# Layer 1's blocks with themselves: a quarter of the scores turned by TensorE, empty places filled, and an end of its own for the last block

## The chip, the cores and the metric

The kernel runs on one core of a Trainium2 chip. The metric is device time in microseconds (us) from the first to the last instruction of one execution; the time of a kernel is the median of its runs. The core's engines work side by side: TensorE (PE) multiplies, and loads weights on a path of its own (PEld); VectorE (DVE), ScalarE (ACT) and GpSimd (POOL) work element by element; transfers are issued on SyncE's queue (SP). Each engine takes its instructions in the order in which the program was built, and waits where one needs what another engine has not yet delivered.

## The reference, cut to what matters

The input x has 4 images of 128 channels and 64 x 64 = 4096 places. Layer 0 is an attention with keys and queries of 64 channels and a gate; layer 1, which the change touches, takes the result as 4096 tokens of 128 channels, attends with queries that are also the keys, and ends in a recurrent step over the tokens.

```python
def _L1_attn_ref(x, W, b):
    q = jnp.einsum('bsd,de->bse', x, W)
    scores = jnp.einsum('bsd,btd->bst', q, q)      # symmetric: q with itself
    attn = jax.nn.softmax(scores, axis=-1)
    return jnp.einsum('bst,btd->bsd', attn, x)

def _L1_ffn_ref(x, W, V, gamma, beta):
    Wx = jnp.einsum('bti,hi->bth', x, W)
    flat = Wx.reshape(B * T, H)                    # mean and variance over all tokens of all images
    mean = jnp.mean(flat, axis=0); var = jnp.var(flat, axis=0)
    Wx = ((flat - mean) * jax.lax.rsqrt(var + BN_EPS) * gamma + beta).reshape(B, T, H)
    def step(yt, wx_t):
        yt = jax.nn.sigmoid(wx_t + yt @ V.T)
        return (yt, yt)
    ...

# layer 0
x = x + _L0_conv_ref(_gn(x), ...)
# layer 1
t = _to_tokens(x)
t = t + _L1_attn_ref(_ln_t(t), L1_attn_W, L1_attn_b)
t = t + _L1_ffn_ref(_ln_t(t), L1_ffn_W, L1_ffn_V, L1_ffn_gamma, L1_ffn_beta)
```

Since layer 1's scores are symmetric, the kernel works out a block of 512 keys by 512 queries once and turns its exponentials for the opposite block. A block with itself holds the same twofold content within the one block.

## The kernel before

The core holds P = 128 partitions; a block has QB = 512 places (NQ = 4 tiles of 128), and there are NB = 8 blocks per image. Small work is cut into steps in two queues: `pending` holds what finishes a block, `ahead` what prepares the next image. In layer 0 the loop takes `ahead` first, and `pending` every second time:

```python
def nothing():
    pass
# ... attention, the loop of layer 0: per pair of key tiles
if ahead:
    ahead.popleft()()
elif pending and (p % 2 == 0 or len(pending) > 6):
    pending.popleft()()
```

Layer 1 goes through blocks n of queries and a <= n of keys. `slots` takes the row sums, one column for each block n; `quarter` and the tile `before` do not exist yet. The blocks with a < n are turned by VectorE and transfers, and used a second time by `reversed_products`:

```python
slots = accp.tile([P, NT, NB], F32, tag="slots", name="slots", bufs=2)
# ...
def order(n):
    return [0, 1] if b == B - 1 and n == 0 else list(range(n, -1, -1))
# ...
def direct():
    n, a, i, e, o = fifo.popleft()
    for half in range(2):
        nc.tensor.matmul(
            o, lhsT=h[:, NQ * a + 2 * i + half, :], rhs=e[:, half, :],
            start=(a == order(n)[0] and i == 0 and half == 0),
            stop=(a == order(n)[-1] and i == 1 and half == 1),
        )
    if a == order(n)[-1] and i == 1:
        part(n, o)
# ...
for n in [NB - 2, NB - 1] + list(range(NB - 3, -1, -1)):
    # ...
    for a in order(n):
        # ...
        for i in range(2):
            ps = ps_s.tile([P, 2, QB], F32, tag="s", name="ps")
            e = ep.tile([P, 2, QB], F32, tag="e", name="e")
            for half in range(2):
                at = NQ * a + 2 * i + half
                nc.tensor.matmul(
                    ps[:, half, :], lhsT=qt[:, bass.ts(at, P)],
                    rhs=qt[:, bass.ts(n, QB)], start=True, stop=True,
                )
            for half in range(2):
                at = NQ * a + 2 * i + half
                nc.scalar.activation(
                    e[:, half, :], ps[:, half, :], AF.Exp, bias=shift,
                    accum_out=slots[:, at, n : n + 1],
                )
                if turns(n, a):
                    nc.vector.transpose(
                        d.rearrange("q f b k j -> q k b f j")[:, 2 * i + half],
                        e[:, half, :].rearrange("q (b f j) -> q b f j", b=NQ, f=NQ),
                    )
            if o is None:
                o = ps_o.tile([P, QB], F32, tag="o", name="o")
            if n == NB - 2 and i == 0 and a > 0:
                queries(a - 1)
            elif n == NB - 2 and a == 0 and i == 1:
                flush((b, NB - 1))
                queries(NB - 1)
            fifo.append((n, a, i, e, o))
            clock += 1
            if len(fifo) > LAG:
                direct()
                if a == n and i == 0:
                    direct()
            if turned and turned[0][0] <= clock:
                reversed_products()
            if pending:
                pending.popleft()()
            elif ahead:
                ahead.popleft()()
        # ... the transfers that turn d into t, and turned.append((clock + 4, n, a, t))
    while fifo:
        direct()
```

A block is finished when all its parts are there. `ps_m` has one bank, so the steps below follow one another on it:

```python
def finish(n):
    cs = bass.ts(n, QB)
    rinv = stat.tile([P, NQ], F32, tag="rinv", name="rinv")
    t = work.tile([P, 4, NQ, 32], F32, tag="t", name="t1", bufs=2)
    h2 = work.tile([P, NQ, C], F32, tag="h2", name="h2")
    th = work.tile([P, QB], F32, tag="th", name="th")
    t1 = work.tile([P, NQ, C], F32, tag="og", name="t1b")
    nc.sync.dma_start(t, t_d[b, n])
    def tokens():
        at = (B + b) * NT + n * NQ
        den = den_all[:, at : at + NQ]
        nc.vector.tensor_reduce(den, slots[:, bass.ts(n, NQ), :], AX.X, ALU.add)
        nc.vector.reciprocal(rinv, den)
        m = ps_m.tile([P, NQ, P], F32, tag="m", name="mt")
        for j in range(NQ):
            nc.tensor.transpose(m[:, j, :], oacc[:, n, bass.ts(j, P)], ident)
        for j in range(NQ):
            nc.vector.scalar_tensor_tensor(
                t1[:, j, :].rearrange("q (p i) -> q p i", p=4),
                m[:, j, :].rearrange("q (p i) -> q p i", p=4), rinv[:, j : j + 1],
                t[:, :, j, :], ALU.mult, ALU.add,
            )
        layernorm(quarters(t1), quarters(h2))
    def result():
        m = ps_m.tile([P, QB], F32, tag="m", name="mr")
        for j in range(NQ):
            nc.tensor.transpose(m[:, bass.ts(j, P)], t1[:, j, :], ident)
        t2 = work.tile([P, QB], F32, tag="xb", name="t2")
        nc.scalar.copy(t2, m)
        nc.sync.dma_start(t2_d[b, :, cs], t2)
    def turn():
        m = ps_m.tile([P, QB], F32, tag="m", name="mh")
        for j in range(NQ):
            nc.tensor.transpose(m[:, bass.ts(j, P)], h2[:, j, :], ident)
        nc.scalar.copy(th, m)
    def inputs():
        m = ps_m.tile([P, QB], F32, tag="m", name="mw")
        nc.tensor.matmul(m, lhsT=wt["f"], rhs=th, start=True, stop=True)
        nc.vector.bn_stats(bn_st[:, b * NB + n, :], m)
        m = m.rearrange("p (g i s) -> p i g s", i=L // 2, s=2)
        # ... copied to wxs, or to DRAM for the images before the last
    if b == B - 1 and n == 0:
        pending.extend([tokens, turn, inputs, result])
    else:
        pending.extend([tokens, result, turn, inputs])
```

After the last block the statistics of all tokens are joined, and the recurrent step runs over 32 groups' starts in parallel. The pool `scan` takes the place in memory of what stood there before:

```python
        flush()
# ...
    with ExitStack() as st:
        scan = st.enter_context(tc.tile_pool(name="scan", bufs=1))
        # ... loads of t2, tiles y and state, first products into the banks of ps_r (line 725)
mv = scan.tile([P, 2], F32, name="bn_mv")
nc.vector.bn_aggr(mv, bn_st.rearrange("p a b -> p (a b)"))
gain = scan.tile([P, 1], F32, name="gain")
inv_sqrt(gain, mv[:, 1:2], EPS_BN)
nc.vector.tensor_mul(gain, gain, col(GAMMA))
bias = scan.tile([P, 1], F32, name="bias")
nc.vector.tensor_mul(bias, mv[:, 0:1], gain)
nc.vector.tensor_sub(bias, col(BETA), bias)
# ...
                nc.scalar.activation(dst, at(wxs, i, bs), AF.Sigmoid, bias=bias, scale=gain)   # line 761
```

## Time and profile before

| What | Value |
|---|---|
| time, median of 3 runs (lowest, highest) | 3108.49 us (3106.8, 3109.73) |
| span of the profiled execution, mean granted clock of TensorE | 3106.2 us, 0.993 |
| GpSimd | 5% busy |
| one 512-column exponential of layer 1 (ScalarE), its read-out of the row sum | 684 ns, 196 ns |
| layer 1 of the second image, 1134 to 1530 us: see the slices from 1200 to 1500, TensorE busy | 98.05 to 98.90 us of each 100 |
| the last slice, 3000 to 3100: TensorE busy, granted clock | 61.80 us of 100, 0.82 |
| chain that ended last: layer 0's products, its scores | 28%, 15% |
| the same: layer 1's scores, direct products, turned products | 15%, 14%, 12% |

How to read the lines that follow: a group shows line, engine, operation, tile written and tiles read, shapes and count, then busy time and the mean duration of one in ns, then the engine's idle time just before it and what ended it. In the timeline the first number is the start in us, the second the length of the piece, and the bracket gives idle time before it with what ended it. TensorE's instructions overlap, and their ends are modelled, so the distance of two starts says more than a duration.

### The profile page before, as it was taken

What the parts mean: (1) busy time and instruction counts of PE and PEld (TensorE: products, weight loads), DVE (VectorE), ACT (ScalarE), POOL (GpSimd) and SP (SyncE); (2) the same over time, 40 slices, a digit from 0 to 9 for tenths busy, and PEclk for the clock granted to TensorE, in tenths of its full rate; (3) what the DMA queues carried; (4) which work ended last, traced back from release to release, by engine and by line L of the source; (5) the groups of instructions that cost most, each with busy time, mean ns of one, the idle gap of its engine ahead of it and who ended that gap; (6) DMA issues with size and microseconds to landing.
All of it is one profiled execution on the core that took longest, in us unless ns stands there. A gap on an engine that the chain in (4) does not pass through costs nothing.

```text
span 3106.2 us, 32252 instructions
## 1 busy us (share of the span) xinstructions
PE 3018.6 (97%) x10706; PEld 1362.3 (44%) x10706; DVE 1877.7 (60%) x3160; ACT 1144.8 (37%) x2018; POOL 144.5 (5%) x183
## 2 busy tenths in 40 slices
PE   7999999999999999999999999999999999999976
PEld 3444444444444444444444444444444444444432
DVE  6666656555666665655566666555566666455546
ACT  3444433333344443333334443333334444323324
POOL 0000000000000000000000000000000000000000
PEclk9999999999999999999999999999999999999988
DMA  1011143333111123334211114333321113443423
GB/s 51 28 55 55 55 111 88 91 89 92 46 55 55 55 78 93 90 89 97 73 52 55 50 43 116 88 91 93 91 56 55 49 44 121 114 104 88 98 98 157
DMA packets 233168, 241.14 MB, mean 78 GB/s; under 512 B 88480, under 2 KB 144288, under 8 KB 231968
## 3 DMA queue, kind: packets, MB, share of 16 engines
q1 hardware_dynamic: 231984, 238.18, 28.2%
q8 instruction: 88, 1.44, 0.2%
q10 hardware_dynamic: 1008, 0.79, 0.1%
q14 instruction: 88, 0.72, 0.1%
HBM read 65.80 MB, written 56.62 MB: 39 GB/s over the span
## 4 chain that ended last, share of the span: by engine, by line
PE 91%; DVE 4%; SPq 1%; POOL 1%; DMA 1%; issue 1%; ACT 0%; ACTq 0%; DVEq 0%; POOLq 0%
PE o L394 28%; PE ps L215 15%; PE ps L613 15%; PE o L501 14%; PE ot L514 12%; SPq L650 1%; PE m L243 1%; PE mw L582 1%; PE mq L487 1%; PE mp L326 1%; PE ps_r L764 1%; PE mh L577 1%; POOL rstd L132 1%; DVE t1b L559 1%; PE mp L361 1%; PE mp L346 1%
## 5 line engine op out<-in xcount | busy, mean ns | idle before, releaser
L394 PE MATMUL o<-e,nxt 64*128 64x512 f32 x4096 | 963.8, 589 | 0.0
L217 ACT ACTIVATE e<-ps 128x1024 f32<-128x1024 f32 x512 | 521.4, 1025 | 674.7 <-PE ps L215 657.5
L224 DVE TENSOR_TENSOR acc<-acc,e 128x1024 f32<-128x1024 f32 x448 | 547.6, 1222 | 236.4 <-ACT e L217 220.5
L619 ACT ACTIVATE e<-ps,shift 128x512 f32<-128x512 f32 x580 | 393.9, 684 | 749.8 <-PE ps L613 497.1
L394 PEld LDWEIGHTS o<-e,nxt 64*128 64x128 f32 x4096 | 399.0, 187 | 482.3 <-issue 474.5
L613 PE MATMUL ps<-qt 128*128 128x512 f32 x1160 | 547.8, 595 | 2.7 <-ACT qt L488 2.7
L501 PE MATMUL o<-e,h 128*128 128x512 f32 x1160 | 537.7, 592 | 0.0
L215 PE MATMUL ps<-nxt 64*128 64x512 f32 x2048 | 534.5, 596 | 1.2 <-DVE nxt L338 0.9
L514 PE MATMUL ot<-tt,h 128*128 128x512 f32 x888 | 399.8, 593 | 0.0
L624 DVE STREAM_TRANSPOSE dd<-e 128x512 f32<-128x512 f32 x444 | 286.5, 686 | 83.4 <-ACT e L619 73.1
L501 PEld LDWEIGHTS o<-e,h 128*128 128x128 f32 x1160 | 218.3, 191 | 260.7 <-issue 259.5
L613 PEld LDWEIGHTS ps<-qt 128*128 128x128 f32 x1160 | 213.4, 191 | 249.0 <-issue 224.2
L215 PEld LDWEIGHTS ps<-nxt 64*128 64x128 f32 x2048 | 194.5, 187 | 231.5 <-issue 158.8
L514 PEld LDWEIGHTS ot<-tt,h 128*128 128x128 f32 x888 | 167.9, 190 | 210.0 <-issue 205.7
L519 DVE TENSOR_REDUCE slots<-tt 128x4 f32<-128x2048 f32 x111 | 250.7, 2258 | 9.7 <-DMA tt<-dd 9.4
L528 DVE TENSOR_TENSOR oacc<-oacc,ot 128x512 f32<-128x512 f32 x87 | 59.3, 682 | 209.8 <-PE ot L514 209.8
L131 POOL TENSOR_SCALAR rstd<-mv 128x4 f32<-128x4 f32 x64 | 14.6, 228 | 2456.5 <-DVE mv L268 2456.5
L619 ACT ACTIVATION_READ_ACCUMULATOR e<-ps,shift 128x1 f32 x580 | 113.9, 196 | 0.0
L448 DVE SCALAR_TENSOR_TENSOR t<-yt,rinv,t 128x128 f32<-128x128 f32 x128 | 36.6, 347 | 71.5 <-DMA yt<-turn_d 71.4
L411 POOL TENSOR_SCALAR xb<-xb,bpc 128x512 f32<-128x512 f32 x32 | 57.4, 1793 | 318.0 <-DMA xb<-in_x_dram 289.3
L132 POOL TENSOR_TENSOR rstd<-rstd,mhalf 128x4 f32<-128x4 f32 x64 | 66.4, 1038 | 5.3
L271 DVE TENSOR_SCALAR h<-t,mv,rstd 128x128 f32<-128x128 f32 x128 | 35.7, 343 | 47.1 <-POOL rstd L132 47.1
(134 smaller groups left out, 1491.7 us busy)
## 6 DMA issues: line engine op xcount, KB each, us to landing
tt<-dd SPq DMA_DIRECT2D x1776, 64.0 KB, 2.0
turn_d<-d SPq DMA_DIRECT2D x96, 256.0 KB, 2.0
t_d<-t SPq DMA_DIRECT2D x64, 256.0 KB, 2.0
nxt<-in_x_dram SPq DMA_DIRECT2D x16, 512.0 KB, 5.5
xb<-in_x_dram SPq DMA_DIRECT2D x32, 256.0 KB, 2.9
t<-turn_d SPq DMA_DIRECT2D x128, 64.0 KB, 2.0
yt<-turn_d SPq DMA_DIRECT2D x128, 64.0 KB, 2.0
qt<-turn_d SPq DMA_DIRECT2D x128, 64.0 KB, 2.0
```

What stands on the lines that cost most here:

```text
L132: nc.gpsimd.tensor_tensor(dst, dst, mhalf[:, :n], ALU.pow)
L215: nc.tensor.matmul(ps[:, h, :], lhsT=lhsT, rhs=rhs, start=True, stop=True)
L217: nc.scalar.activation(e, ps, AF.Exp, scale=scale)
L224: nc.vector.tensor_tensor(acc, acc, e, ALU.add)
L394: nc.tensor.matmul(o[r], lhsT=v[rs, p + h * PAIRS, :], rhs=e[rs, h, :], start=(p == 0 and h == 0), stop=(p == PAIRS - 1 and h == 1),)
L501: nc.tensor.matmul(o, lhsT=h[:, NQ * a + 2 * i + half, :], rhs=e[:, half, :], start=(a == order(n)[0] and i == 0 and half == 0), stop=(a = ...
L514: nc.tensor.matmul(ot, lhsT=h[:, NQ * n + j, :], rhs=t[:, :, j, :, :].rearrange("q p k j -> q k p j"), start=(j == 0), stop=(j == NQ - 1),)
L519: nc.vector.tensor_reduce(slots[:, bass.ts(n, NQ), a], t.rearrange("q p b k j -> q b p (k j)"), AX.XY, ALU.add,)
L528: nc.vector.tensor_tensor(oacc[:, n, :], oacc[:, n, :], o, ALU.add)
L613: nc.tensor.matmul(ps[:, half, :], lhsT=qt[:, bass.ts(at, P)], rhs=qt[:, bass.ts(n, QB)], start=True, stop=True,)
L619: nc.scalar.activation(e[:, half, :], ps[:, half, :], AF.Exp, bias=shift, accum_out=slots[:, at, n : n + 1],)
L624: nc.vector.transpose(d.rearrange("q f b k j -> q k b f j")[:, 2 * i + half], e[:, half, :].rearrange("q (b f j) -> q b f j", b=NQ, f=NQ),)
```

## The change

It has five parts. (1) In a block with itself the second pair of key tiles is handled by `quarter`: only its second half of the queries is multiplied; its first half is turned by TensorE from the exponentials of the first pair, and ScalarE copies it out of PSUM with a row sum into one more column of `slots`. The purpose is to replace two products of 256 columns by four transposes. (2) Two empty places stand between `result` and `turn` of a finished block, and an empty place now runs a step of `ahead`, if there is one; the purpose is that `turn` finds its layernorm done. (3) What is left from layer 1 is taken one step per pair in layer 0. (4) The last block of the last image has tiles and banks of its own for its end, and its `tokens` come first. (5) The small tiles of the statistics move to the pool that outlives the stage, and one early sigmoid brings its table.

```diff
--- before.py
+++ after.py
@@ -164,6 +164,10 @@
     keep = keep_ctx.enter_context(tc.tile_pool(name="keep", bufs=1))
     bn_st = keep.tile([P, B * NB, 6], F32, name="bn_st")
     den_all = keep.tile([P, 2 * B * NT], F32, name="den_all")
+    mv = keep.tile([P, 2], F32, name="bn_mv")
+    gain = keep.tile([P, 1], F32, name="gain")
+    bias = keep.tile([P, 1], F32, name="bias")
+    first_y = keep.tile([P, 1], F32, name="first_y")
     with ExitStack() as st:
         big = st.enter_context(tc.tile_pool(name="big", bufs=1))
@@ -181,7 +185,10 @@
         pending: deque = deque()
         def nothing():
-            pass
+            if ahead:
+                ahead.popleft()()
         done = set()
@@ -195,6 +202,7 @@
             fifo: deque = deque()
             o = None
+            left = len(pending)
             def pop():
                 nonlocal o
@@ -229,7 +237,8 @@
                             pop()
                     if ahead:
                         ahead.popleft()()
-                    elif pending and (p % 2 == 0 or len(pending) > 6):
+                    elif pending and (p % 2 == 0 or left > 0 or len(pending) > 6):
+                        left -= 1
                         pending.popleft()()
             while fifo:
                 pop()
@@ -472,7 +481,8 @@
             dd = big.tile([P, 2, NQ, NQ, NQ, 32], F32, tag="dd", name="dd")
             tt = big.tile([P, 3, NQ, NQ, NQ, 32], F32, tag="tt", name="tt")
-            slots = accp.tile([P, NT, NB], F32, tag="slots", name="slots", bufs=2)
+            slots = accp.tile([P, NT, NB + 1], F32, tag="slots", name="slots", bufs=2)
+            nc.gpsimd.memset(slots[:, :, NB:], 0.0)
             fifo: deque = deque()
             turned: deque = deque()
             clock = 0
@@ -486,6 +496,34 @@
                 moved = qt[:, cs].rearrange("c (p j k) -> c j p k", j=NQ, p=4)
                 nc.tensor.matmul(m, lhsT=wt["a"], rhs=moved, start=True, stop=True)
                 nc.scalar.copy(qt[:, cs], m)
+            def quarter(n, ps, e, before, slots):
+                hb = QB // 2
+                for half in range(2):
+                    nc.tensor.matmul(
+                        ps[:, 0, bass.ts(half, hb)], lhsT=qt[:, bass.ts(NQ * n + 2 + half, P)],
+                        rhs=qt[:, n * QB + hb : (n + 1) * QB], start=True, stop=True,
+                    )
+                for half in range(2):
+                    for c in range(2):
+                        nc.tensor.transpose(
+                            ps[:, 1, bass.ts(2 * half + c, P)],
+                            before[:, c, bass.ts(2 + half, P)], ident,
+                        )
+                for half in range(2):
+                    at = NQ * n + 2 + half
+                    nc.scalar.activation(
+                        e[:, half, hb:], ps[:, 0, bass.ts(half, hb)], AF.Exp, bias=shift,
+                        accum_out=slots[:, at, n : n + 1],
+                    )
+                for half in range(2):
+                    at = NQ * n + 2 + half
+                    nc.scalar.activation(
+                        e[:, half, :hb], ps[:, 1, bass.ts(half, hb)], AF.Identity,
+                        accum_out=slots[:, at, NB : NB + 1],
+                    )
             def order(n):
@@ -542,9 +580,22 @@
                 cs = bass.ts(n, QB)
                 rinv = stat.tile([P, NQ], F32, tag="rinv", name="rinv")
                 t = work.tile([P, 4, NQ, 32], F32, tag="t", name="t1", bufs=2)
-                h2 = work.tile([P, NQ, C], F32, tag="h2", name="h2")
-                th = work.tile([P, QB], F32, tag="th", name="th")
-                t1 = work.tile([P, NQ, C], F32, tag="og", name="t1b")
+                if b == B - 1 and n == 0:
+                    one, two = (ep.tile([P, 2, QB], F32, tag="e", name="last") for _ in range(2))
+                    h2, t1 = (one[:, r, :].rearrange("q (j c) -> q j c", j=NQ) for r in range(2))
+                    th, t2 = two[:, 0, :], two[:, 1, :]
+                    def bank():
+                        return ps_s.tile([P, 2, QB], F32, tag="s", name="ml")[:, 0, :]
+                else:
+                    h2 = work.tile([P, NQ, C], F32, tag="h2", name="h2")
+                    th = work.tile([P, QB], F32, tag="th", name="th")
+                    t1 = work.tile([P, NQ, C], F32, tag="og", name="t1b")
+                    t2 = None
+                    def bank():
+                        return ps_m.tile([P, QB], F32, tag="m", name="m1")
                 nc.sync.dma_start(t, t_d[b, n])
                 def tokens():
@@ -552,7 +603,7 @@
                     den = den_all[:, at : at + NQ]
                     nc.vector.tensor_reduce(den, slots[:, bass.ts(n, NQ), :], AX.X, ALU.add)
                     nc.vector.reciprocal(rinv, den)
-                    m = ps_m.tile([P, NQ, P], F32, tag="m", name="mt")
+                    m = bank().rearrange("q (j c) -> q j c", j=NQ)
                     for j in range(NQ):
                         nc.tensor.transpose(m[:, j, :], oacc[:, n, bass.ts(j, P)], ident)
                     for j in range(NQ):
@@ -564,21 +615,23 @@
                     layernorm(quarters(t1), quarters(h2))
                 def result():
-                    m = ps_m.tile([P, QB], F32, tag="m", name="mr")
+                    nonlocal t2
+                    m = bank()
                     for j in range(NQ):
                         nc.tensor.transpose(m[:, bass.ts(j, P)], t1[:, j, :], ident)
-                    t2 = work.tile([P, QB], F32, tag="xb", name="t2")
+                    if t2 is None:
+                        t2 = work.tile([P, QB], F32, tag="xb", name="t2")
                     nc.scalar.copy(t2, m)
                     nc.sync.dma_start(t2_d[b, :, cs], t2)
                 def turn():
-                    m = ps_m.tile([P, QB], F32, tag="m", name="mh")
+                    m = bank()
                     for j in range(NQ):
                         nc.tensor.transpose(m[:, bass.ts(j, P)], h2[:, j, :], ident)
                     nc.scalar.copy(th, m)
                 def inputs():
-                    m = ps_m.tile([P, QB], F32, tag="m", name="mw")
+                    m = bank()
                     nc.tensor.matmul(m, lhsT=wt["f"], rhs=th, start=True, stop=True)
                     nc.vector.bn_stats(bn_st[:, b * NB + n, :], m)
                     m = m.rearrange("p (g i s) -> p i g s", i=L // 2, s=2)
@@ -590,9 +643,12 @@
                         nc.sync.dma_start(wxs_d[b, :, :, bass.ts(n, GB), :], wx)
                 if b == B - 1 and n == 0:
-                    pending.extend([tokens, turn, inputs, result])
+                    pending.appendleft(tokens)
+                    pending.extend([result, turn, inputs])
+                elif b == B - 1 and n < 4:
+                    pending.extend([tokens, result, turn, inputs])
                 else:
-                    pending.extend([tokens, result, turn, inputs])
+                    pending.extend([tokens, result, nothing, nothing, turn, inputs])
             for n in [NB - 2, NB - 1] + list(range(NB - 3, -1, -1)):
@@ -608,23 +664,27 @@
                     for i in range(2):
                         ps = ps_s.tile([P, 2, QB], F32, tag="s", name="ps")
                         e = ep.tile([P, 2, QB], F32, tag="e", name="e")
-                        ... (lines 611 to 627 as they stand above)
+                        if a == n and i == 1:
+                            quarter(n, ps, e, before, slots)
+                        else:
+                            ... (the same lines, one step further in)
+                        before = e
                         if o is None:
                             o = ps_o.tile([P, QB], F32, tag="o", name="o")
                         if n == NB - 2 and i == 0 and a > 0:
@@ -700,6 +760,8 @@
                 ahead.popleft()()
         flush()
+        nc.scalar.activation(first_y, shift, AF.Sigmoid)
         ok = big.tile([P, 2, 2 * B * NT], F32, tag="oacc", name="ok")
         nc.vector.tensor_scalar(ok[:, 0, :], den_all, DEN_LO, None, ALU.is_ge)
         nc.vector.tensor_scalar(ok[:, 1, :], den_all, DEN_HI, None, ALU.is_le)
@@ -726,13 +788,10 @@
                     banks[s][i][:, : HB * G], lhsT=ident, rhs=wxs[:, 0, :HB, :, 0],
                     start=True, stop=True, skip_group_check=True,
                 )
-        mv = scan.tile([P, 2], F32, name="bn_mv")
         nc.vector.bn_aggr(mv, bn_st.rearrange("p a b -> p (a b)"))
-        gain = scan.tile([P, 1], F32, name="gain")
         inv_sqrt(gain, mv[:, 1:2], EPS_BN)
         nc.vector.tensor_mul(gain, gain, col(GAMMA))
-        bias = scan.tile([P, 1], F32, name="bias")
         nc.vector.tensor_mul(bias, mv[:, 0:1], gain)
         nc.vector.tensor_sub(bias, col(BETA), bias)
```

More of the change, by code (lines that the diff above doesn't have):

```diff
@@ L610, in layer1 @@
                         e = ep.tile([P, 2, QB], F32, tag="e", name="e")
-                        for half in range(2):
-                            at = NQ * a + 2 * i + half
-                            nc.tensor.matmul(
-                                ps[:, half, :], lhsT=qt[:, bass.ts(at, P)],
-                                rhs=qt[:, bass.ts(n, QB)], start=True, stop=True,
-                            )
-                        for half in range(2):
-                            at = NQ * a + 2 * i + half
-                            nc.scalar.activation(
-                                e[:, half, :], ps[:, half, :], AF.Exp, bias=shift,
-                                accum_out=slots[:, at, n : n + 1],
-                            )
-                            if turns(n, a):
-                                nc.vector.transpose(
-                                    d.rearrange("q f b k j -> q k b f j")[:, 2 * i + half],
-                                    e[:, half, :].rearrange("q (b f j) -> q b f j", b=NQ, f=NQ),
-                                )
+                        if a == n and i == 1:
+                            quarter(n, ps, e, before, slots)
+                        else:
+                            for half in range(2):
+                                at = NQ * a + 2 * i + half
+                                nc.tensor.matmul(
+                                    ps[:, half, :], lhsT=qt[:, bass.ts(at, P)],
+                                    rhs=qt[:, bass.ts(n, QB)], start=True, stop=True,
+                                )
+                            for half in range(2):
+                                at = NQ * a + 2 * i + half
+                                nc.scalar.activation(
+                                    e[:, half, :], ps[:, half, :], AF.Exp, bias=shift,
+                                    accum_out=slots[:, at, n : n + 1],
+                                )
+                                if turns(n, a):
+                                    nc.vector.transpose(
+                                        d.rearrange("q f b k j -> q k b f j")[:, 2 * i + half],
+                                        e[:, half, :].rearrange("q (b f j) -> q b f j", b=NQ, f=NQ),
+                                    )
+                        before = e
                         if o is None:
```

## The prediction

> **What bounds the kernel now.** I read the engine shares first, then the chain that ended last, then the groups of instructions, then what TensorE waits for, and last the timeline of the end.
>
> ```profile
> PE 3018.6 (97%) x10706; PEld 1362.3 (44%) x10706; DVE 1877.7 (60%) x3160; ACT 1144.8 (37%) x2018; POOL 144.5 (5%) x183
> ...
> PE 91%; DVE 4%; SPq 1%; POOL 1%; DMA 1%; issue 1%; ACT 0%; ACTq 0%; DVEq 0%; POOLq 0%
> ```
>
> The second line is the chain: 91% of it is TensorE. VectorE and ScalarE have 40% and 63% to spare. So only three things can move the time: fewer or shorter passes on TensorE, fewer stops of TensorE, or a shorter end, where TensorE is not the bound.
>
> The groups give the price of a pass. The count of layer 1's scores, line 613, is 1160 for 580 calls: a product in f32 takes two passes. The transposes of line 557 are 128 for 128 calls (32 places of 4): one pass.
>
> ```profile
> L613 PE MATMUL ps<-qt 128*128 128x512 f32 x1160 | 547.8, 595 | 2.7 <-ACT qt L488 2.7
> L557 PE MATMUL mt<-ident,oacc 128*128 128x128 f32 x128 | 19.9, 278 | 0.0
> ```
>
> The means of 595 and 278 ns overlap with their neighbours and are not the price. The distance from start to start is, and the weight loads show it, since each is issued when the pass before it begins:
>
> ```profile
> 2990.07 0.19 PEld L501 LDWEIGHTS o<-e,h 128*128 128x128 f32 x1 [0.24 <-issue]
> 2990.50 0.14 PEld L557 LDWEIGHTS mt<-ident,oacc 128*128 128x128 f32 x1 [0.24 <-issue]
> 2990.93 0.36 PEld L557 LDWEIGHTS mt<-ident,oacc 128*128 128x128 f32 x3 [0.29 <-issue]
> ```
>
> A 512-column pass is 0.43 us. Four transposes stand in the timeline as one piece of 0.60 us; less the 0.27 of the last one, three distances take 0.33, so 0.11 each.
>
> What TensorE waits for, over the whole span (us in total, times, longest):
>
> ```profile
> PE gm L303 <- DVE gmv L301: 16.3, 1, 16.3
> PE mh L577 <- DVE h L271: 15.7, 21, 4.4
> PE ps_r L764 <- ACT y L761: 7.8, 1, 7.8
> ...
> PE mh L577 <- ACT e L619: 2.8, 3, 1.0
> ```
>
> The first is the start of the program, the third the end. The two for `mh` lie in layer 1: `turn` transposes h2 before the layernorm has finished it. One of them, 4.4 us, is in the end; 14.1 us in 23 stops are left. The profile counts idle time from the modelled end of the pass before (0.59 us after its start), though the next could start after 0.43, so each stop costs 0.16 more: 14.1 + 23 x 0.16 = 17.8 us.
>
> The end, in order of time:
>
> ```profile
> 3001.45 0.66 PE L557 MATMUL mt<-ident,oacc 128*128 128x128 f32 x4
> 3006.50 1.15 PE L577 MATMUL mh<-ident,h 128*128 128x128 f32 x4 [4.39 <-DVE h L271]
> 3015.81 1.02 DVE L730 BATCH_NORM_AGGREGATE bn_mv<-bn_st 128x2 f32<-128x192 f32 x1 [4.03 <-DMA t_d<-t]
> 3018.81 1.28 ACT L761 ACT_TABLE_LOAD   x1 [5.24 <-DVE bias L737]
> 3020.10 1.12 ACT L761 ACTIVATE y<-wxs,bias,gain 128x256 f32<-128x256 f32 x2
> ```
>
> The last block's `tokens` wait until the block before has gone through the one bank `m`; then the statistics over the batch wait for a DMA's landing; then the sigmoid's table is loaded. After 3020.10 come 86.1 us of scan and output.
>
> **What the skill says.** "Perfetto Trace Analysis", Transposes, asks for real transposes in place of a matmul by identity because arithmetic is skipped. The trace agrees in count: one pass where a product has two. "TensorE: Matmul & The Clock Gate", Part 4, gives about 275 ns for a transpose in a kernel's context. The recorded mean here is 278, but back to back they start 0.11 us apart, and that is what I use. "ScalarE: Activation LUTs", What ACT_TABLE_LOAD costs, gives 1283 ns for the load, which the trace shows as 1.28, and some 1380 ns of drain, which the 3018.81 to 3020.10 above does not show. No page that I found says how a program's order is shifted when it is built, and this trace shows that it is: the line 725 products, written after the flush, run at 2997, ahead of line 577's.
>
> **The quarter.** There are 8 blocks with themselves in each of 4 batches, 32 in all (the last batch's block 0 is among them). Each loses two products of 512 columns, 4 passes of 0.43 = 1.72 us. It gains two of 256 columns and 4 transposes. The 256-column pass is line 725's: six in 1.52 us, less one's 0.396, are 0.225 each. So 4 x 0.225 + 4 x 0.11 = 1.34, and I put 0.05 for the seams between kinds: 1.39. The gain is 0.33 x 32 = 10.5 us, all of it on TensorE's own chain.
>
> The transposes need both exponentials of the tile before. With the products of the block before in between (two `direct` calls, 8 passes, 3.4 us) and two exponentials of 0.68 us plus 0.2 of read-out, they should be ready. ScalarE pays: four instructions on 256 columns (line 768's take 489 ns) with four read-outs in place of two of 684, 4 x 0.489 - 2 x 0.684 = 0.6 us more a block and 0.4 for two more read-outs, 32 us in all on an engine with over half its time free. The score banks are two; the tile's bank is needed two steps later, some 5 us, and ScalarE takes about 2.5.
>
> **The empty places.** Two are put between `result` and `turn`, some 3.4 us of TensorE's work each. The layernorm takes 4.6 us from `mt`'s start to the normalisation and 1.1 more, so every `turn` that has them finds h2 ready. They aren't wasted: an empty place now runs a step of the next batch's preparation. In the last batch blocks 3 to 1 keep the old order; the one long stop there, at 2983, is 1.0 us. So 16.8 us can go. The gaps inside `mh` (four normalisations arriving one after another) may give 2 more; new waits at the shifted steps and four more switches per batch between layer 0's half-array products and full ones (in the start times of the trace line 394's pass is 0.1 us longer when a transpose follows) may take 2 back. I put 16.
>
> **The own end.** With `tokens` of the last block first and other banks for it, `mt` can start at 2997.1, when the last sum into oacc is there, not at 3001.45: 4.3 us, of which I give back 0.5 because VectorE also has the other block's statistics and copy then. The copy that follows the last statistics ended at 3011.8, so 3008.0 now, and with mean, gain and bias in the pool that outlives the stage the aggregation need not wait for the landing: 7.8 us earlier than 3015.81. The table in place early takes away 1.3: from bias ready at 3018.7 the activation starts at once. Together 9.1 us. The loads of t2s, which took until 3039.07 and were first used at 3041.2, must move too: they wait for the last result's landing and the release of the old tiles, which I put at 3007, 9 us earlier. So they stay hidden.
>
> **The sum.** 10.5 + 16 + 9 = 35.5, and 1.5 back for leftovers in layer 0, taken one to a pair now, where `result` may come before VectorE has finished t1: 34 us, 3108.5 - 34 = 3074.5. I say 3074.
>
> **Rivals.** First, the transposes could become the new `mh`: a TensorE in strict order waiting for ScalarE. At 0.8 us, like the long stops of `mh`, 32 of them would cost 26 us, eat the gain of the quarter and give about 3100. For it: the order fixed when the program is built misjudged h2. Against it: h2 hung on VectorE and GpSimd in turn, while the products of line 501, which hang on the same exponentials, show 0.0 idle in 1160 passes. Second, the stops may move, not go: the preparation steps now stand in the gap, share the one bank `m`, and VectorE is their engine; then the empties bring 5 in place of 16: 3085. Third, in the end the loads of t2s could start no earlier than now and hold the additions, or the early sigmoid could be put far forward by the reordering and its table be lost to the exponentials; 3 to 6 us less gain, 3079. Fourth, the weight loads: a 0.19 us load fits under a 0.225 pass, a 0.14 one does not fit under 0.11; if seams cost 0.2 in place of 0.05 the quarter brings 5.5: 3079.
>
> **Range and chances.** Each of the three parts has a sound start in the trace, and the likely errors are losses of some of a gain: quarter 4 to 13, empties 8 to 20, end 5 to 11. Not all fall short together: 3063 to 3090. Faster by over 2% needs 3046, 28 us below my number, more than all waits named; slower by over 2% needs new waits of 100 us. 0.02, 0.97, 0.01.
>
> **What would show it.** The score passes of layer 1 split into 1160 - 128 = 1032 of 512 columns and 128 of 256, and 128 transposes of e on a line of their own, with little idle before it. The two `mh` rows should shrink below 3 us. First activation of the scan near 3020 less 34, without a table load before it, and 86 us from there to the end. I am wrong if a wait of TensorE for e or for the banks of the scores stands among the longest, if `mr` or `mp` inherits the waits of `mh`, or if the aggregation still waits for a landing.

## The result, and the profile after

The changed kernel takes 3069.98 us (median of 4 runs, 3067.95 to 3070.61), the kernel before in the same comparison 3107.64 (3106.76 to 3109.73): a ratio of 0.9877, 95% interval 0.986 to 0.9894. The profiled execution spans 3066.1 us, 40.1 less than the one of before. 3074 had been predicted, within 3063 to 3090.

The page of the changed kernel, engine shares and the chain that ended last:

```profile
PE 3000.1 (98%) x10834; PEld 1377.5 (45%) x10834; DVE 1882.3 (61%) x3160; ACT 1154.7 (38%) x2148; POOL 148.3 (5%) x187
...
PE 95%; DVE 3%; ACT 1%; POOL 0%; DMA 0%; issue 0%; ACTq 0%; SPq 0%; DVEq 0%; POOLq 0%
```

TensorE has 128 instructions more and is still the bound: 95% of the chain in place of 91%. Its busy time fell by only 18.5 us, since that number counts the modelled length of a pass and not the distance of two.

The groups on TensorE that answer to the score passes, from the list by shape:

```profile
L672 PE MATMUL ps<-qt 128*128 128x512 f32 x1032 | 490.9, 595 | 2.9 <-ACT qt L498 2.7
L505 PE MATMUL ps<-qt 128*128 128x256 f32 x128 | 32.9, 379 | 0.0
...
L511 PE MATMUL ps<-ident,e 128*128 128x128 f32 x128 | 19.4, 273 | 0.0
```

These are the 1032, 128 and 128 that were foretold. The transposes of e have no idle time before them: the exponentials are always there. In the start times of the trace a 256-column pass is followed after 0.216 us (median of 128) and a transpose after 0.110, its last one included.

What TensorE waits for now (us in total, times, longest):

```profile
PE gm L312 <- DVE gmv L310: 15.9, 1, 15.9
PE n_ok L147 <- DVE par_ok L850: 5.5, 1, 5.5
PE ps L672 <- ACT qt L498: 2.7, 4, 0.7
PE mp L335 <- DVE nxt L347: 2.5, 3, 0.8
PE ml L630 <- DVE last L280: 2.5, 1, 2.5
PE ps_r L823 <- DVE ps_r L810: 2.3, 10, 0.2
PE ps L223 <- ACT e L225: 2.2, 1, 2.2
...
PE m L630 <- DVE h L280: 1.8, 3, 0.6
```

The stops at the transposes of h2 (`m` from h, line 630) went from 18.5 us in 24 (4.4 of it in the end) to 1.8 in 3, all three in the last image, and 2.5 in the end (`ml` from last, the same transposes of the last block). Two rows are to be kept in mind: `mp`, products of the next image's preparation, and `ps L223`, a stop in layer 0. The kernel before has two rows of the first kind:

```profile
PE mp L346 <- DVE nxt L351: 2.4, 3, 0.8
PE mp L326 <- DVE nxt L351: 2.4, 3, 0.8
```

That is one stop at the products for the values (line 346) and one at those for queries and keys (line 326) in each layer 1 of the first three images; one of the two is left.

The end of the changed kernel in order of time:

```profile
2967.26 0.66 PE L608 MATMUL ml<-ident,oacc 128*128 128x128 f32 x4 [1.66 <-DVE oacc L566]
2972.90 1.10 PE L630 MATMUL ml<-ident,last 128*128 128x128 f32 x4 [2.47 <-DVE last L280]
2977.99 1.01 DVE L791 BATCH_NORM_AGGREGATE bn_mv<-bn_st 128x2 f32<-128x192 f32 x1
2980.91 1.28 ACT L820 ACT_TABLE_LOAD   x1 [6.29 <-DVE bias L796]
2982.20 1.12 ACT L820 ACTIVATE y<-wxs,bias,gain 128x256 f32<-128x256 f32 x2
```

The last block's `tokens` start as soon as the last sum is there, and the aggregation follows the last statistics without a wait. But the table is still loaded at 2980.91. The early sigmoid is elsewhere; ScalarE at the start of the program shows it:

```profile
7.26 1.28 ACT L764 ACT_TABLE_LOAD   x1 [7.26 <-DMA w<-in_wts_dram]
8.56 0.20 ACT L764 ACTIVATE first_y<-shift 128x1 f32<-128x1 f32 x1
...
29.34 1.28 ACT L225 ACT_TABLE_LOAD   x1
30.64 1.94 ACT L225 ACTIVATE e<-ps 128x1024 f32<-128x1024 f32 x2
```

It depends on a constant alone and was built into the first idle place, so the exponentials have to load their table in front of the first products of layer 0, and TensorE stops there (`ps L223`).

Cutting both traces at the first score pass of each layer, at the start of the last direct pass and at the first activation of the scan gives the account of the 40 us:

| Stretch | before, us | after, us | difference |
|---|---|---|---|
| up to layer 0 of image 1 | 27.3 | 26.9 | -0.4 |
| layer 0 of image 1 | 366.0 | 369.4 | +3.5 |
| layer 1 of images 1 to 3, each | 391.0 | 380.7 | 3 x -10.3 |
| layer 0 of images 2 to 4, each | 351.5 | 352.3 | 3 x +0.8 |
| layer 1 of image 4 up to the last direct pass | 373.5 | 369.3 | -4.3 |
| from there to the first activation of the scan | 25.7 | 17.6 | -8.1 |
| scan and output | 86.1 | 83.9 | -2.1 |

A stretch can be split further into work and waiting. Work is every pass of TensorE at its back-to-back distance (0.429 us for 512 columns, 0.216 for 256, 0.110 for a transpose, 0.423 for a pair of half-array passes); the rest is waiting, switches between kinds of passes included. For layer 1 of image 2, the changed kernel and the runs of the next section:

| Kernel | length | work | waiting |
|---|---|---|---|
| before | 391.0 | 380.1 | 10.9 |
| after | 380.7 | 376.35 | 4.4 |
| without the quarter | 381.85 | 379.7 | 2.2 |
| without the empty places | 386.4 | 376.8 | 9.6 |
| the quarter alone | 387.3 | 376.8 | 10.5 |
| empty places that stay idle | 378.5 | 372.9 | 5.6 |
| steps spread, sigmoid tied | 379.5 | 376.35 | 3.2 |

The quarter takes 3.3 us of work from an image (0.41 in each of 8 blocks), as the passes say, with the empty places or without. How much waiting goes with it is another matter.

### The profile page after: what moved, and what is told of

It is laid out like the page before. It is cut to its first block, busy times and chain, and to the rows that moved or that the text cites. A ratio compares the mean times of both kernels' runs of the same rounds, so it can differ in the third digit from the quotient of the medians.

```text
span 3066.1 us, 32642 instructions
## 1 busy us (share of the span) xinstructions
PE 3000.1 (98%) x10834; PEld 1377.5 (45%) x10834; DVE 1882.3 (61%) x3160; ACT 1154.7 (38%) x2148; POOL 148.3 (5%) x187
## 4 chain that ended last, share of the span: by engine, by line
PE 95%; DVE 3%; ACT 1%; POOL 0%; DMA 0%; issue 0%; ACTq 0%; SPq 0%; DVEq 0%; POOLq 0%
PE o L403 29%; PE o L539 16%; PE ps L223 15%; PE ps L672 14%; PE ot L552 12%; PE m L252 1%; PE m L635 1%; PE mq L497 1%; PE ps L505 1%; PE mp L335 1%; PE mp L370 1%; PE mp L355 1%; DVE ps_r L810 1%; DVE t2s L837 1%; PE m L630 1%; PE m L608 0%
## 5 line engine op out<-in xcount | busy, mean ns | idle before, releaser
L678 ACT ACTIVATE e<-ps,shift 128x512 f32<-128x512 f32 x516 | 350.4, 683 | 670.0 <-PE ps L672 506.1
L223 PE MATMUL ps<-nxt 64*128 64x512 f32 x2048 | 535.8, 597 | 2.2 <-ACT e L225 2.2
L672 PE MATMUL ps<-qt 128*128 128x512 f32 x1032 | 490.9, 595 | 2.9 <-ACT qt L498 2.7
L223 PEld LDWEIGHTS ps<-nxt 64*128 64x128 f32 x2048 | 194.4, 187 | 231.2 <-issue 158.9
L672 PEld LDWEIGHTS ps<-qt 128*128 128x128 f32 x1032 | 187.8, 190 | 213.0 <-issue 188.0
L678 ACT ACTIVATION_READ_ACCUMULATOR e<-ps,shift 128x1 f32 x516 | 101.3, 196 | 0.0
```

Of the source, the lines that this page charges most:

```text
L223: nc.tensor.matmul(ps[:, h, :], lhsT=lhsT, rhs=rhs, start=True, stop=True)
L672: nc.tensor.matmul(ps[:, half, :], lhsT=qt[:, bass.ts(at, P)], rhs=qt[:, bass.ts(n, QB)], start=True, stop=True,)
L678: nc.scalar.activation(e[:, half, :], ps[:, half, :], AF.Exp, bias=shift, accum_out=slots[:, at, n : n + 1],)
```

## The experiments

All times are medians; the kernel before was between 3107.5 and 3110.2 us in these comparisons, and the unaltered changed kernel, measured in two of them, 3069.98 and 3067.69. So a difference of medians from two comparisons can be off by some 2 us. The lengths from one layer's start to the next agree to 0.2 us in the two profiles of the changed kernel, and carry the finer readings. The experiments alter the changed kernel, unless another is named.

**Without the quarter.** The blocks with themselves are multiplied in full.

```diff
-                        if a == n and i == 1:
+                        if False:
                             quarter(n, ps, e, before, slots)
```

> The changed kernel with the quarter taken out: the blocks with themselves are multiplied in full, all else stays. Theory (the gain is TensorE's passes: 4 x 0.429 us less 4 x 0.216 and 4 x 0.110, 0.41 us in each of 32 blocks): 13.2 us slower than the changed kernel, about 3083, and each layer 1 of the first three images 3.3 us longer (380.7 to 384.0). Rival (the other order of the program is what helps, or the transposes wait for ScalarE and eat the gain): less than 7 us.

Measured: 3074.63 us, 0.9892 of before (0.9875 to 0.9908). That is 4.7 us slower than the changed kernel, not 13.2: by the bar set there, the rival. Yet the work is longer by 3.3 us an image, as the theory had it. What it missed is in the waits of TensorE of this run:

```profile
PE ps L672 <- ACT qt L498: 2.7, 4, 0.7
PE ml L630 <- DVE last L280: 2.5, 1, 2.5
PE ps_r L823 <- DVE ps_r L810: 2.3, 10, 0.2
PE ps L223 <- ACT e L225: 2.2, 1, 2.2
PE m L630 <- DVE h L280: 2.1, 3, 0.8
```

Between the first line and the last the row `mp L335 <- DVE nxt L347` of the changed kernel is missing. With the quarter, layer 1 waits 2.2 us an image more. The transposes of e don't wait for ScalarE (0.0 idle ahead of line 511 above). In the start times 1.9 of the 2.2 us lie at the products `mp` of line 335, for the next image's queries and keys: 1.0 in one stop and the rest in pieces of 0.1 to 0.2.

**The cut alone.** The same four pieces of 256 columns, but products in place of the transposes, and exponentials in place of the copies.

```diff
-                    for c in range(2):
-                        nc.tensor.transpose(
-                            ps[:, 1, bass.ts(2 * half + c, P)],
-                            before[:, c, bass.ts(2 + half, P)], ident,
-                        )
+                    nc.tensor.matmul(
+                        ps[:, 1, bass.ts(half, hb)], lhsT=qt[:, bass.ts(NQ * n + 2 + half, P)],
+                        rhs=qt[:, n * QB : n * QB + hb], start=True, stop=True,
+                    )
...
-                        e[:, half, :hb], ps[:, 1, bass.ts(half, hb)], AF.Identity,
+                        e[:, half, :hb], ps[:, 1, bass.ts(half, hb)], AF.Exp, bias=shift,
```

> The changed kernel with the second pair of a block with itself cut into the same four 256-column pieces, but with products in place of the transposes, and exponentials in place of the copies. Theory (passes alone): 8 x 0.216 = 1.73 us against 1.28, so 0.45 x 32 = 14 us slower than the changed kernel, about 3084, and the same as the kernel without the quarter within 2 us. Rival (what helps is the finer cut, since ScalarE and the banks get smaller pieces): near the changed kernel, within 4 us of 3070.

Measured: 3076.18 us, 0.9893 (0.9876 to 0.9909), 1.6 from the kernel without the quarter. So the finer pieces bring nothing; what the quarter brings, it brings by one-pass transposes in place of two-pass products. The size is off in the same way as above: layer 1 of image 2 has 379.75 us of work and 2.8 of waiting.

**The quarter alone**, put into the kernel before with its column of `slots` and nothing else of the change.

> The kernel before with the quarter alone (and the column of slots it needs). Theory (the parts add up): 13.2 us faster than before, about 3094.5, layer 1 of the first three images 391.0 to 387.7, with the stops at the transposes of h2 as before. Rival (the quarter needs the empty places): under 7 us faster, with new idle time ahead of the transposes of e.

Measured: 3091.64 us, 0.9944 (0.9927 to 0.9961), 18.2 us less than before in the same comparison (15.1 by the profiled spans). Layer 1 of the first three images is 386.7, 387.3 and 386.6. The stops at h2 remain, as the waits show:

```profile
PE mh L606 <- DVE h L271: 14.6, 21, 4.4
PE ps_r L797 <- ACT y L794: 7.8, 1, 7.8
PE n_ok L147 <- DVE par_ok L824: 5.5, 1, 5.5
PE ps L645 <- ACT qt L489: 2.7, 4, 0.7
PE mp L326 <- DVE nxt L351: 2.4, 3, 0.8
```

The rival, that the quarter needs the empty places, falls. Here it took about 1 us of waiting off (10.9 to 9.9 in image 1, 10.5 in image 2): of the two rows `mp` of the kernel before, the one of line 346 is gone. The same edit is thus worth 15 to 18 us in one kernel and 5 to 6 in the other, for the same 13 us of work. In the first it took away a stop at `mp`, in the second it brought one.

**Without the empty places.**

```diff
-                    pending.extend([tokens, result, nothing, nothing, turn, inputs])
+                    pending.extend([tokens, result, turn, inputs])
```

> The changed kernel without the two empty places (tokens, result, turn, inputs as before), all else stays. Theory (turn finds h2 unfinished without them): the long stops of TensorE at the transposes of h2 come back, 17 to 20 us slower, about 3088, layer 1 of the first three images 6 to 7 us longer (380.7 to 387). Rival (the stops had gone already because the quarter shifts the order): under 6 us slower.

Measured: 3084.6 us, 0.992 (0.9904 to 0.9937), 14.6 us slower (16.5 by the spans), layer 1 of images 1 to 3 at 386.4. The waits of TensorE:

```profile
PE gm L312 <- DVE gmv L310: 15.8, 1, 15.8
PE m L630 <- DVE h L280: 11.7, 23, 0.7
```

The stops at h2 are back in all 23 places, a little shorter than before. The theory stands, with a size somewhat under its range.

**Empty places that stay idle.**

```diff
         def nothing():
-            if ahead:
-                ahead.popleft()()
+            pass
```

> The changed kernel with empty places that do nothing. Theory (the distance between result and turn is what helps; the next image's preparation has room later in layer 1 anyway): within 2 us of the changed kernel, near 3070. Rival (filling matters: the preparation is left over and is emptied in a heap between the layers): 5 us or more slower, with the waits at the transitions from layer 1 to layer 0.

Measured: 3079.38 us, 0.9901 (0.9885 to 0.9918), 9.4 us slower. My theory falls here: the distance is not enough, the filling counts. Layer 1 even gets shorter, 378.5, but layer 0 of images 2 to 4 grows from 352.3 to 358.2: four products for the gates (8 passes) of the next image no longer fit into layer 1 and are emptied at the border, where they run between half-array passes. Both layers of an image together are 3.6 us longer. 0.8 of it is the eight passes themselves, which start 0.53 us apart there and 0.43 in layer 1; the rest is waiting and switches between kinds of passes. Three images make 10.9. Some stops at h2 return as well:

```profile
PE m L627 <- DVE h L277: 4.1, 9, 0.6
```

**Without the early sigmoid** (its line left out), and **with the sigmoid tied** to a sum that exists only after the last exponential:

```diff
-        nc.scalar.activation(first_y, shift, AF.Sigmoid)
+        nc.scalar.activation(first_y, den_all[:, (2 * B - 1) * NT + NQ : (2 * B - 1) * NT + NQ + 1], AF.Sigmoid)
```

> The changed kernel without the early sigmoid. Theory (the sigmoid was built into the very start of the program, where it takes the table, so that the exponentials load theirs at 29.3 us and TensorE stops and then runs cold): the first image's layer 0 is back from 369.4 to 366.0 us, 3.5 us faster than the changed kernel, about 3066.5; a table load stays at the end. Rival (that stretch is longer for another reason, such as the other order of the first steps): no difference over 1 us.

> The changed kernel with the early sigmoid reading the last block's sums, so that it can't stand before the last exponential. Theory: the 3.5 us of the start come back and the table is loaded in idle time of the end, which brings 1.3 more: 4.8 us faster than the changed kernel, about 3065, and no table load between bias and the first activation of the scan. Rival (the load in the end delays the copies there and gives the 1.3 back): 3.5 us, as without it.

Measured: 3066.71 us, 0.9867 (0.9851 to 0.9884), without it; 3066.21, 0.9864 (0.9848 to 0.9881), tied. In both, layer 0 of image 1 is back at 365.96 us to the hundredth: the early sigmoid cost 3.5 us in the change as made. The granted clock tells the second half of that. Windows of the changed kernel, ahead of, in and after the stop (TensorE's clock is the third number from the end):

```profile
26.90:28.90 2.00, 2.00 (x8) 1.09 (x8) 1.94 (x4) 0.20 (x1) 0.00 (x0) 1.00 0.00 0
28.90:31.70 2.80, 0.62 (x2) 0.00 (x0) 1.80 (x4) 2.77 (x4) 0.00 (x0) 1.00 0.00 0
31.70:34.90 3.20, 3.18 (x8) 1.34 (x10) 2.23 (x3) 2.67 (x3) 0.00 (x0) 0.55 0.00 0
```

After 2.2 us of idleness TensorE ran at half its clock for 3.4 us, from 32.0 to 35.4 (the third window, with a mean of 0.55, begins 0.3 us earlier). The run with the statistics in the scan's pool, below, had the same stop and no such dip, and its layer 0 is 367.85: about 1.9 us for the stop, 1.6 for the clock.

Tied, the table is loaded at 2959.63, in ScalarE's idle time. The medians are 0.5 us apart, and the two kernels' runs overlap; the stretches say the same more surely. From the end of the last direct pass to the first activation it is 16.84 us in place of 18.14, 1.3 less, but scan and output take 84.71 in place of 83.88, so 0.8 is given back. ScalarE at the start of the scan, tied:

```profile
2980.50 1.12 ACT L820 ACTIVATE y<-wxs,bias,gain 128x256 f32<-128x256 f32 x2 [6.30 <-DVE bias L796]
2982.82 0.49 ACT L827 ACTIVATE y<-ps_r,bias 128x256 f32<-128x256 f32 x1 [1.19 <-PE ps_r L823]
```

The first activation comes 0.1 us after bias is ready (2980.42), as the theory had it. The activation behind these two then waits 1.19 us for TensorE: it comes 2.32 us after the first, and without the sigmoid 1.45. TensorE in this time, tied and then without the sigmoid:

```profile
2977.80 4.53 PE L787 MATMUL ps_r<-wxs,ident 128*128 128x256 f32 x12 [1.47 <-DVE wxs L639]
2982.16 1.69 PE L823 MATMUL ps_r<-y,w 128*128 128x256 f32 x5
```

```profile
2976.90 4.44 PE L786 MATMUL ps_r<-wxs,ident 128*128 128x256 f32 x12 [1.47 <-DVE wxs L639]
2981.60 2.25 PE L822 MATMUL ps_r<-y,w 128*128 128x256 f32 x7 [0.26 <-issue]
```

Without the sigmoid the twelve products into the scan's banks are done when y arrives; tied, TensorE is still at them, most of them at half its clock (0.50 up to 2980.5; they start 0.43 us apart there, and 0.23 at the full clock). So with the table out of the way these products are the next limit, and they take two thirds of the 1.3 back. That is close to the rival's number, for a different reason: no copy was delayed.

**Without the own end**, and **statistics in the scan's pool**. In the first the last block uses the common tiles and the one bank, in the old order, while mean, gain and bias stay in the pool that outlives the stage; in the second it is the other way round.

```diff
-                if b == B - 1 and n == 0:
+                if False:
...
-                    pending.appendleft(tokens)
-                    pending.extend([result, turn, inputs])
+                    pending.extend([tokens, turn, inputs, result])
```

```diff
-    mv = keep.tile([P, 2], F32, name="bn_mv")
-    gain = keep.tile([P, 1], F32, name="gain")
-    bias = keep.tile([P, 1], F32, name="bias")
...
+        mv = scan.tile([P, 2], F32, name="bn_mv")
+        gain = scan.tile([P, 1], F32, name="gain")
+        bias = scan.tile([P, 1], F32, name="bias")
```

> The changed kernel without tiles, banks and order of its own for the last block; the statistics' tiles stay in the pool that outlives the stage. Theory (two savings: the last block's start 4.3 us earlier, and no wait for a landing, worth 4): only the first is lost, 4 us slower than the changed kernel, about 3074, with 19 us from the last sum into oacc to the scan. Rival (the wait for the landing is what counted, and the last block's start is hidden by it): no difference over 1.5 us.

> The changed kernel with mean, gain and bias back in the pool of the scan; the own end stays. Theory (with its own end the last result is sent off 4 us before the last statistics, so the pool is free in time): within 1.5 us of the changed kernel, near 3070. Rival (the pool is what counted): 3 to 5 us slower, with the aggregation waiting for a landing.

Measured: 3075.62 us, 0.9897 (0.988 to 0.9913), without the own end, 5.6 slower, against the 4 that were expected; 3069.39, 0.9877 (0.986 to 0.9893), with the statistics in the scan's pool, no difference that the runs can tell. From the end of the last direct pass to the first activation it is 25.1 us before, 17.0 after, 22.05 without the own end, 16.8 with the statistics in the pool. So of the 8.1 the own end carries 5 alone; the pool's 3 is there only where the own end is not, and is worth nothing beside it, since the last result then lands before the last statistics are taken. The extra 1.1 us without the own end is this wait in another place: bias is ready at 2985.2, but y lies in the scan's pool too, and the table load ahead of it starts at 2986.38, right behind the landing of the last result at 2986.25.

**At the old pace in layer 0** (`left > 0 or` left out).

> The changed kernel without the faster pace in layer 0 for what layer 1 left over. Theory (the steps are the same and each finds what it needs; the pace only keeps the shared tiles apart): within 1 us of the changed kernel, near 3070. Rival (at the old pace leftovers meet the first finished block of layer 0 on the shared tiles og, h2, xb, and TensorE waits): 2 to 6 us slower in layer 0 of the last three images (352.3 us each).

Measured: 3068.75 us, 0.9871 (0.9855 to 0.9888). By the medians that is the theory's number. But layer 0 of images 2 to 4 is 352.8, 352.8 and 353.3 in place of 352.3, 2.1 us in all and just the rival's least, and the total hides it: layer 0 of image 1 happened to be 1.6 us shorter here, without the dip of the clock. The waits show three new stops:

```profile
PE ps L223 <- ACT e L225: 3.0, 4, 2.2
```

They stand at the start of layer 0, 2 us after its first pass, where TensorE waits 0.27 us for an exponential. With the 0.16 us that a stop costs besides, they make 1.3 of the 2.1 us. At the tiles that the rival named, og, h2 and xb, no wait of TensorE shows. So the faster pace is worth about 2 us, but not for the rival's reason.

**Steps spread, and the changed kernel again on the same chip.** In the changed kernel two products for queries and keys stand in a row, and the second must wait for the one bank m, which three operations of VectorE and ScalarE hold one after another. TensorE of the changed kernel there:

```profile
1210.95 1.02 PE L335 MATMUL mp<-nxt,w 128*128 128x512 f32 x2
1211.81 1.88 PE L672 MATMUL ps<-qt 128*128 128x512 f32 x4
1214.53 1.12 PE L335 MATMUL mp<-nxt,w 128*128 128x512 f32 x2 [0.84 <-DVE nxt L347]
```

Spread, with the sigmoid tied:

```diff
-                ahead.extend(norm + sum(chunks, []) + gates)
+                spread, late = [], []
+                for n0, n1, k0, k1, v0, v1 in chunks:
+                    spread += [n0] + late + [k0, n1, v0, k1]
+                    late = [v1]
+                ahead.extend(norm + spread + [nothing_more] + late + gates)
```

> The changed kernel with the tied sigmoid, and with the next image's steps spread: two products for queries and keys no longer stand in a row, a step without the bank m is between. Theory (the quarter's missing gain went into stops of TensorE at these products, 1.0 us at one place of each layer 1 and some smaller ones, because the bank is held through three operations): layer 1 of the first three images 380.7 to about 379, without a stop of 1.0 us at about 84 us, 5 us less than the tied sigmoid alone would give, about 3061 against 3066. Rival (the built order shifts and other steps inherit the wait, as with the products for the values in the kernel before): layer 1 within 0.7 us of 380.7, time within 2 us of 3066.

> The changed kernel unaltered, on the same chip as the run with spread steps, so that the two can be set side by side: 3070 within 2 us, layer 1 of the first three images 380.7, layer 0 of the first 369.4 or, where TensorE's clock recovers one window sooner, 367.9.

Measured: 3062.73 us (3062.25 to 3063.13), 0.9857 (0.9841 to 0.9873), spread and tied; 3067.69 (3065.78 to 3068.59), 0.9871 (0.9854 to 0.9887), the changed kernel. On one chip the version that is spread and tied is 5.0 us faster than the changed kernel, and their runs don't overlap; against the tied kernel alone, from another comparison, it is 3.5, about three times the 1.2 us that each layer 1 gets shorter. The same place in it:

```profile
1205.24 1.02 PE L338 MATMUL mp<-nxt,w 128*128 128x512 f32 x2
1206.10 3.60 PE L675 MATMUL ps<-qt 128*128 128x512 f32 x8
1209.53 1.05 PE L358 MATMUL mp<-w,nxt 128*128 128x128 f32 x8
```

The stop is gone, and layer 1 is 379.5 us, 1.2 shorter at the same work. It is the fastest of the kernels here, by about 45 us against the one before. The theory holds for 1.2 us of the 2.2 that the quarter lost in an image; the other 1.0 lies at the same products `mp`, in pieces of 0.1 to 0.2 us in the start times, and what ends each was not tried.

## Why the prediction was right, and where it was not

**The sum** was 34 us less; measured were 37.7 by the medians, 40.1 by the profiles. The direction, the size and the bound were right, but not each term, and that the total fell so near is in part luck. The quarter and the empty places together were put at 26.5 us, and layer 1 of the four images gave 35.1. Against that stand the 3.5 that the early sigmoid cost and some smaller errors. The two parts also don't add in one way. By the profiles the quarter gives 15.1 us where there are no empty places and 6.4 where there are. The empty places take 5.6 us off a layer 1 that has the quarter (386.4 to 380.7), and with the quarter out layer 1 stands 9.2 us below the kernel before (391.0 to 381.85), since there both stops at `mp` are gone too. The prediction added two terms that share what they save.

**The quarter**, put at 10.5 us. Its working was right in kind and the term too small: a 256-column pass is 0.216 us, not the 0.225 taken from the end of the program, and the seam, put at 0.05, is nothing, so the work saved is 0.41 x 32 = 13.2. The step that failed is "all of it on TensorE's own chain". With the empty places in, 2.2 us an image came back as waiting in the first three images and about 1 in the last, and taking the quarter out cost 4.7 us by the medians, 6.4 by the profiles. Most of the rest of the 13.2 went into stops at `mp`, which hang on VectorE, ScalarE and the one bank m, and not on TensorE's chain. The first rival, TensorE waiting for the exponentials, is refuted by the 0.0 idle of line 511.

**The empty places**, put at 16 us. 14.6 were measured by leaving them out (16.5 by the profiles). Two assumptions under the number did not hold as put. That every `turn` with empty places finds h2 ready holds in the first three images; in the last, where `ahead` is empty, blocks 5 and 4 still stop for 0.8 us each. In the built order VectorE's part of block 5's `tokens` stands at 2834.0 there, 20 us after its transposes, `mr` follows at 2835.7 and `mh` at 2838.7; what put it so late was not tried. And "they aren't wasted" said too little: unfilled they give back 9.4 us. The second rival, that preparation steps inherit the waits, is not borne out: the one stop at `mp` of 1.0 us an image stands just so in the kernel without the empty places (2.5 us in 3), it is missing in the one without the quarter, and the kernel before had two.

**The own end**, put at 9.1 us. 8.1 were measured. `mt`'s 4.3 us and the landing's wait were read rightly and, in sum, worth 8; the 1.3 of the table did not come, because the sigmoid was built to the start of the program. The third rival had named that shift, with the table lost to the exponentials and 3 to 6 us less gain: it cost 3.5 us in layer 0 of image 1, by a second table load and the clock after it, besides the gain that did not come. The loads of t2s stayed hidden, as predicted.

**The 1.5 us for leftovers in layer 0** were 0.8 in each of three images, 2.3; 0.4 of each is one `turn` that moved there from layer 1, so no loss.

**Not foreseen**: scan and output got 2.1 us shorter with the same instructions. About 1 us of it lies ahead of the output, all of it in the first nine activations of the scan, and goes with TensorE's clock. In the kernel before it was 0.50 at the start of the scan, in the changed one the twelve products into the scan's banks run just ahead of it, and it is 1.00. Windows, before and then after:

```profile
3020.10:3022.00 1.90, 1.23 (x3) 1.04 (x4) 0.51 (x2) 1.12 (x2) 0.00 (x0) 0.50 0.98 423
```

```profile
2982.20:2984.00 1.80, 1.43 (x6) 0.59 (x4) 0.87 (x2) 1.48 (x3) 0.00 (x0) 1.00 1.00 428
```

The rest lies in the last transfers (25.2 us from the first issue to the last landing before, 23.7 after), for which the change gives no reason.

## What to carry to other kernels

On a saturated engine with a fixed order, passes saved are certain, but the time saved is not: shorter work shifts the small users of a single shared buffer against each other, and the same edit can take a stop away in one kernel and bring one in another. So savings that were estimated one by one should not be added. After such a change read the engine's waits again, and space the steps that hold the buffer longest. An operation without a real dependency, such as an activation meant to bring a table early, is placed wherever the built order has room; give it an input that exists only when it should run.

## What the runs showed of the hardware that I had not expected

- Transposes cost no seam between products of the full array: four of 128 x 128 in f32 behind two-pass products of 256 columns take 0.44 us in all, and the next product follows the last one after 0.11 to 0.13. Next to the half-array passes of layer 0 there is one: such a pass takes 0.52 us in place of 0.42 when a transpose follows.
- One stop of 2.2 us at the start of layer 0 could put TensorE's clock to half for the next 3.4 us (1.6 us lost), or leave it at full, with the same first steps of the program around it: 369.3 to 369.5 us for that layer in seven kernels, 367.85 in two. The traces suggest what decides. All changes of the granted clock fall on a grid of 3.41 us that starts at another moment in each execution; in the seven the grid step before the dip had TensorE idle for 50 to 64% of its length, in the two the grid cut the stop in two and no step reached more than 42%. That was not tried, and in the ends of the kernels the same share does not tell the two cases apart.
- A table load taken off the critical path was worth 0.5 us and not its 1.28, since TensorE, at half its clock until 0.65 us into the scan, was then not done with the products ahead of it.
